# Two graph layers on one core: the order of work taken from a model of time for all engines

## The chip, the cores and the metric

The kernel runs on one core of one Trainium2 chip. The metric is device time in microseconds of one execution. Within the core, TensorE (PE) does the matrix products and transposes, ScalarE (ACT) the exponentials, Gelu and most copies out of PSUM, VectorE (DVE) masks, products, sums and statistics, GpSimd (POOL) a power of -1/2 on small tiles and the issue of one kind of load, and SyncE (SP) issues the other loads and the stores. Each engine takes its instructions in the order in which they were written, so the order of writing is the schedule.

## What is computed

Sixteen graphs of 1024 nodes with 256 features go through two layers. Layer 0 is graph attention with 4 heads of 64 features; layer 1 is masked attention with 8 heads of 32 features and an MLP 256 to 1024 to 256. Cut to what matters:

```python
# layer 0
h = einsum('bnd,hde->bhne', x, W)
weight = leaky_relu(sum over t of (adj == t+1) * (e_src[t][:, None] + e_dst[t][None, :]))
attention = softmax(where(adj == 0, -1e9, weight))
out = layernorm_per_head(relu(attention @ h + bias) + h)
x = layernorm(x + out)
# layer 1
n = layernorm(x) * gamma1 + beta1          # serves as query, key and value
a = softmax(where(adj > 0, n @ n.T / sqrt(32), -inf)) @ n
x1 = x + a
y = layernorm(x1) * gamma2 + beta2
x = layernorm(x + x1 + gelu(y @ W1 + b1) @ W2 + b2)
```

With the adjacency of these inputs only one edge type occurs, and the kernel uses this (a general path exists for other inputs and isn't taken).

## The kernel before

The work is two streams of instructions, written as Python generators. A step of a stream writes some instructions and yields a number, its cost in microseconds of PE time as the author reckoned it.

*Stream 0, layer0,* goes over the 16 batches. First `prepare`: for pairs of node blocks of 128 rows it transposes x (`transpose_rows`, L259, copied by ACT L262), transposes the adjacency into a byte mask (`turn_mask`, L327 on PE, L328 on ACT), multiplies with the weights (L354), lets ACT take parts of the product (L355 to L360), and leaves the value tile to a small chain, `values0` (L378, L379 on DVE). Then `attention0`: 16 steps, each for one half of the nodes (512 queries), one head and four key blocks; `weights` (L406, four DVE instructions) for the next step are written just after the products (L421) of this one. Once in two heads `spread_factor` (L395 on PE, L397 on ACT) makes a factor for the next pair. After the last step of a head two chains begin: `divide0` (L456 on DVE, L459 on ACT) and `after0` (L467 to L537), which adds h, normalises each pair of heads, and at the fourth head adds x, normalises the row, transposes it and leaves what layer 1 needs: x1, the values v1 and the transposed keys nT.

*Stream 1, layer1,* is one batch behind. `attention1` has 32 steps, each for 512 queries, four heads and one key block: `exponentials` writes four logit products into four PSUM banks (L559) and four exponentials (L564), `masked` multiplies the step before with the mask (L570, two DVE instructions), and `products` (L577, L584) takes the step before that one. After the eighth key block, `heads_out` (L619 to L635) divides and transposes, and after the second group of heads `finish1` (L646 to L664) adds x1, takes the statistics of four blocks (L225, L226), a power on POOL (L220), scales on ACT (L236) and transposes into yT. Then `mlp`: L682 on PE with Gelu L689 on ACT, L696 on PE for the chunk before, and one chain `last_norm` (L728 to L738) for each block of 128 rows, which ends with the store.

*What sets the order.* Three things. `COURSE` says how far layer 0 should be at each point of layer 1 (from 1.0 batch ahead at the start to 1.45 at the end of attention 1 and to 2.0 some 18 units before the end of the MLP); the main loop writes the next step of layer 0 if it is behind that course, otherwise of layer 1. The chains stand aside: a chain's part yields a wait, and `advance` writes its next part once the reckoned clock has moved that far. `complete` writes all that is left of a chain at once, where its result or its PSUM bank is needed: `bank0` does this for the readers of one of the two side banks, `finish_norms` for the norms of a half. `half(1)`, first needed at the fifth step of attention 1, is such a place.

The PSUM pools are `ps_s` (four banks), `ps_a` (two side banks, acc0 and acc1) and `ps_o` (two).

Of the kernel before, what the change touches and what calls it, by code (L numbers as in the profile page):

```python
# [31 lines left out]
F32 = mybir.dt.float32  # L32
# [7 lines left out]
P = 128  # L40
# [8 lines left out]

@with_exitstack  # L50
def fast_path(
# [24 lines left out]
    nc = tc.nc  # L76
# [23 lines left out]
    one = ctx.enter_context(tc.tile_pool(name="one", bufs=1))  # L100
    two = ctx.enter_context(tc.tile_pool(name="two", bufs=2))
    three = ctx.enter_context(tc.tile_pool(name="three", bufs=3))
    four = ctx.enter_context(tc.tile_pool(name="four", bufs=4))
    six = ctx.enter_context(tc.tile_pool(name="six", bufs=6))
    small = ctx.enter_context(tc.tile_pool(name="small", bufs=3))
    ps_s = ctx.enter_context(tc.tile_pool(name="ps_s", bufs=4, space=PSUM))
    ps_a = ctx.enter_context(tc.tile_pool(name="ps_a", bufs=1, space=PSUM))
    ps_o = ctx.enter_context(tc.tile_pool(name="ps_o", bufs=2, space=PSUM))
# [7 lines left out]
    make_identity(nc, ident)  # L116
# [73 lines left out]

    def later_weights():
# [5 lines left out]
        yield 6.0  # L197
        nc.sync.dma_start(w1_sb, w1.rearrange("(c p) f -> p c f", p=P))
        nc.sync.dma_start(w2_sb, w2.rearrange("(c p) d -> p c d", p=P))
        yield 24.0  # L200
# [11 lines left out]
        yield 3.5  # L212
# [10 lines left out]
    def statistics(src, mv):  # L223
        st = small.tile([P, 6], F32, name="st")
        nc.vector.bn_stats(st, src)  # L225
        nc.vector.bn_aggr(mv, st)  # L226
# [14 lines left out]
    def bank0(shape, dtype=F32):  # L241
# [4 lines left out]
        return ps_a.tile(shape, dtype, name=f"acc{i}"), banks0[i]  # L246
# [26 lines left out]
    clock = [0.0]  # L273
    chains = []

    def begin(chain, wait):
        chains.append([clock[0] + wait, chain])

    def run(item):
        wait = next(item[1], None)  # L280
        if wait is None:
            chains.remove(item)
        else:
            item[0] = clock[0] + wait

    def advance(cost):
        clock[0] += cost
        for item in list(chains):
            if item[0] <= clock[0]:
                run(item)  # L290

    def complete(chain):

        for item in list(chains):
            if item[1] is chain:
# [22 lines left out]
    def prepare(b, hb, esr, v0, dinv, mask):  # L318
# [18 lines left out]

        for k in range(0, NB, GB):
# [5 lines left out]
            yield 0.45  # L344
            turn_mask(k)
            yield 0.5
# [4 lines left out]
            for g in range(GB):  # L351
                ph, bank = bank0([P, D + 2 * H0])
# [5 lines left out]
                bank["readers"] = [values0(v0[:, k + g, :, :], ph)]  # L358
                begin(bank["readers"][0], 1.0)
                nc.scalar.copy(hb[-1][:, (k + g) % BPH, :], ph[:, 0:D])  # L360
                yield 0.9
                if g == 0:
                    turn_mask(k + 1)
                    yield 0.5
            turning = turn_sources(esr[:, k * P : (k + GB) * P])
# [903 lines left out]
```

## Time and profile before

| | before |
|---|---|
| median of three runs | 3697.59 us (3694.15 to 3701.16) |
| the profiled execution | 3704.23 us |
| its span | 3702.3 us |
| its mean granted PE clock | 0.978 |
| instructions | 142339 |
| first part, layer 0 of batch 0 alone | 0 to about 145 us |
| last part, layer 1 of batch 15 alone | from about 3523 us |

Profile lines give, for a chain row, the start in us, the length in us, the engine, the tile and the line of the kernel, and the number of records merged. Each fp32 product has two records. A line of waits names who waited for whom, then the total in us, the number of times and the longest. A busy PE is not a PE at its peak, since matmuls overlap in the record.

### The profile page before, as it was taken

Reading aid. Unit: us, or ns where it says so; the run is one execution under the profiler, and the core shown is the slowest. Engines: PE = TensorE matmul, PEld = TensorE weight load, DVE = VectorE, ACT = ScalarE, POOL = GpSimd, SP = SyncE. Lnnn points to the kernel's source line nnn. Section 1 sums busy time; section 2 is a strip of 40 time slices with the busy share of each in tenths; the row PEclk is TensorE's granted clock in tenths of the full one; section 3 lists DMA queues with packets and bytes.
Section 4 is the critical chain, followed back from the end, with each engine's and each line's share of the span. In section 5 each row is a group of like instructions: output and inputs, shape, how many; then the busy total and the mean of one; then the engine's idle time right before and its main releaser. Section 6 shows DMA issues by size and latency. Waiting matters only on the chain.

```text
span 3702.3 us, 142339 instructions
## 1 busy us (share of the span) xinstructions
PE 3487.3 (94%) x64673; PEld 2358.5 (64%) x64673; DVE 2857.4 (77%) x4882; ACT 2274.1 (61%) x5084; POOL 410.2 (11%) x392
## 2 busy tenths in 40 slices
PE   6799999999999999999999999999999999999998
PEld 5457576575756758566575765757657575675846
DVE  6787786877778787787877878788787877878774
ACT  3655757567475664757657475575756747566464
POOL 1101011010110101011020110101101011010100
PEclk9899999999999999999999999999999999999999
DMA  4101102011020110201102010110201102010000
GB/s 101 36 14 29 33 12 43 8 33 28 14 45 7 38 23 19 42 11 36 17 25 37 11 39 14 29 33 12 43 8 36 26 13 46 6 37 9 15 7 14
DMA packets 77525, 97.30 MB, mean 26 GB/s; under 512 B 9072, under 2 KB 59760, under 8 KB 76912
## 3 DMA queue, kind: packets, MB, share of 16 engines
q0 software_dynamic: 18432, 33.56, 6.4%
q1 hardware_dynamic: 56896, 53.50, 4.7%
q8 instruction: 508, 8.32, 0.9%
q10 hardware_dynamic: 1584, 1.05, 0.1%
q14 instruction: 105, 0.86, 0.1%
HBM read 104.87 MB, written 16.78 MB: 33 GB/s over the span
## 4 chain that ended last, share of the span: by engine, by line
PE 76%; DVE 16%; ACT 6%; issue 2%; DMA 0%; POOL 0%; ACTq 0%; POOLq 0%; DVEq 0%
PE ps L559 17%; PE po L577 13%; PE acc L421 11%; PE po L696 9%; PE ps L682 8%; PE po L584 7%; DVE p L406 3%; PE acc L354 3%; DVE st L225 2%; PE acc L259 2%; PE acc L327 2%; DVE p L570 1%; ACT relu L459 1%; DVE mv L226 1%; DVE o L646 1%
## 5 line engine op out<-in xcount | busy, mean ns | idle before, releaser
L570 DVE TENSOR_TENSOR p<-p,mask 128x1024 f32<-128x1024 f32 x1024 | 1202.7, 1220 | 245.1 <-ACT p L564 240.7
L564 ACT ACTIVATE p<-ps 128x512 f32<-128x512 f32 x2048 | 1071.1, 632 | 286.3 <-PE ps L559 283.2
L559 PE MATMUL ps<-nT 32*128 32x512 f32 x4096 | 761.7, 648 | 24.4 <-ACT cb L397 17.2
L406 DVE SCALAR_TENSOR_TENSOR p<-cb,dinv,mask 128x512 f32<-128x512 f32 x1024 | 698.4, 744 | 6.8 <-ACT cb L397 6.8
L421 PE MATMUL acc<-v,p 128*64 128x65 f32 x16384 | 575.6, 228 | 71.4 <-DVE p L406 63.4
L421 PEld LDWEIGHTS acc<-v,p 128*64 128x64 f32 x16384 | 526.6, 141 | 148.3 <-DVE p L406 71.8
L584 PEld LDWEIGHTS po<-v,p 128*32 128x32 f32 x32768 | 396.4, 110 | 321.1 <-issue 238.0
L577 PE MATMUL po<-p,v 128*32 128x512 f32 x2048 | 550.7, 613 | 2.4 <-DVE p L570 2.4
L577 PE MATMUL po<-p,unit 128*32 128x512 f32 x2048 | 550.0, 613 | 0.0
L682 PE MATMUL ps<-yT,w_sb 128*128 128x256 f32 x2048 | 487.5, 386 | 0.0
L696 PE MATMUL po<-w_sb,hid 128*128 128x256 f32 x2048 | 480.0, 385 | 0.0
L689 ACT ACTIVATE hid<-ps,b_sb 128x256 f32<-128x256 f32 x512 | 233.1, 474 | 351.2 <-PE ps L682 350.7
L682 PEld LDWEIGHTS ps<-yT,w_sb 128*128 128x128 f32 x2048 | 380.5, 191 | 64.5 <-issue 11.4
L696 PEld LDWEIGHTS po<-w_sb,hid 128*128 128x128 f32 x2048 | 386.1, 192 | 54.2
L584 PE MATMUL po<-v,p 128*32 128x33 f32 x32768 | 390.2, 198 | 4.2 <-issue 3.3
L559 PEld LDWEIGHTS ps<-nT 32*128 32x128 f32 x4096 | 265.4, 186 | 186.6 <-ACT p L564 62.0
L577 PEld LDWEIGHTS po<-p,v 128*32 128x32 f32 x2048 | 78.4, 108 | 371.6 <-DVE p L570 202.0
L220 POOL TENSOR_TENSOR r<-v,mhalf 128x1 f32<-128x1 f32 (+1 forms) x160 | 148.5, 928 | 756.8 <-DVE v L732 304.2
L328 ACT ACTIVATE mask<-acc,shift_c 128x1024 uint8<-128x1024 bf16 x128 | 148.1, 1157 | 82.3 <-PE acc L327 81.8
L220 POOL TENSOR_TENSOR r<-v1s,mhalf 128x4 f32<-128x4 f32 x32 | 61.9, 1933 | 1171.5 <-DVE v1s L651 1171.5
L459 ACT ACTIVATE relu<-acc,ranges 128x64 f32<-128x64 f32 x512 | 119.1, 323 | 109.2 <-DVE ranges L456 109.2
L236 ACT ACTIVATE z<-z,t,r 128x256 f32<-128x256 f32 x128 | 81.6, 638 | 162.2 <-DVE t L230 160.7
(121 smaller groups left out, 3087.6 us busy)
## 6 DMA issues: line engine op xcount, KB each, us to landing
ak<-in_adj_dram POOLq DMA_DIRECT2D x128, 256.0 KB, 3.9
xk<-in_x_dram SPq DMA_DIRECT2D x64, 256.0 KB, 2.8
xl<-in_x_dram SPq DMA_DIRECT2D x32, 512.0 KB, 3.9
out_dram<-z SPq DMA_DIRECT2D x128, 128.0 KB, 1.7
w_sb<-in_L_gnn_W_dram SPq DMA_DIRECT2D x2, 1024.0 KB, 6.7
v<-in_L_gnn_a_src_dram SPq DMA_DIRECT2D x2, 320.0 KB, 4.7
v<-in_L_gnn_a_dst_dram ACTq DMA_DIRECT2D x1, 320.0 KB, 4.5
xl<-in_L_gnn_a_dst_dram ACTq DMA_DIRECT2D x1, 320.0 KB, 4.7
```

What stands on the lines that cost most here:

```text
L220: nc.gpsimd.tensor_tensor(r, src, mhalf[:, :n], op=OP.pow)
L406: nc.vector.scalar_tensor_tensor(p[:, i, :], cb[:, hd % PAIR, :], dinv[:, j2 + i, hd : hd + 1], mask[n][:, j2 + i, :], op0=OP.max, op1=OP. ...
L421: nc.tensor.matmul(av[at : at + TILE, q, :], ps[i // 2][:, i % 2, q * P + at : q * P + at + TILE], v0[:, j4 + i, hd, :], start=j4 + i == 0 ...
L459: nc.scalar.activation(t[:, q, :], av[:, q, 0:HO], AF.Relu, scale=rinv[:, q : q + 1])
L559: nc.tensor.matmul(tiles[e], of_keys[q, quad, keys], of_queries[q, quad, :], start=True, stop=True)
L564: nc.scalar.activation(p[:, i, :], tiles[e + i], AF.Exp, scale=SCALE1)
L570: nc.vector.tensor_mul(p, p, mask[n][:, jb, None, :].to_broadcast([P, PAIR, HALF]))
L577: nc.tensor.matmul(moved[at * Q : (at + 1) * Q, :], v, ps[0][:, e, :], start=jb == 0, stop=jb == NB - 1)
L584: nc.tensor.matmul(held[at : at + Q, q, e, :], ps[1][:, e, q * P + at : q * P + at + Q], values[:, hd, :], start=jb == 0 and e == 0 and q ...
L682: nc.tensor.matmul(ph, w1_sb[:, c, f * P : (f + 1) * P], yT[:, c, q * P : (q + GB) * P], start=c == 0, stop=c == DC - 1,)
L689: nc.scalar.activation(hid[f // 4][:, f % 4, :], ph, AF.Gelu, bias=b1_sb[:, f : f + 1], scale=1.0)
L696: nc.tensor.matmul(po, hid[f // 4][:, f % 4, g * P : (g + 1) * P], w2_sb[:, f, :], start=f == 0, stop=f == FC - 1,)
```

## The change

No operation is removed or added; what is written on the engines is the same work in another order. `nc` becomes a `Pace`, which passes every instruction on to the real `nc` and keeps, in Python, a reckoned time for each engine: when it is free, when each tile is written, and when it was last read. The costs are formulas for each engine. `Ring` stands for a tile pool: it knows which tiles are still in use, and before a buffer is taken again it completes the chains that use the old tile.

A chain's part no longer yields a wait but the engine it will run on, and what it needs: tiles, or functions that give a time. `advance` writes it once these are ready by the time that the engine gets there. A stream's step yields its cost, as before, and what its next step needs; the main loop follows the same `COURSE`, but takes the other stream where the chosen one is late by over 0.3 us more than the other, as long as layer 0 stays within `SLACK` (0.12 of a batch) of the course.

```diff
+class Ring:
+    def tile(self, shape, dtype, name, passing=False):
+        taken = self.taken.setdefault(name, [])
+        if len(taken) >= self.bufs:
+            self.pace.settle(taken[-self.bufs])
...
+    def ready(self, name, count=1):
+        taken = self.taken.get(name, [])
+        return max([self.pace.through(t) for t in taken[-self.bufs :][:count] if len(taken) >= self.bufs] + [0.0])
...
+class Pace:
+    LATENCY = {"tensor": 0.2, "scalar": 0.2, "vector": 0.12, "gpsimd": 0.2, "sync": 4.0}
...
+    def cost(self, engine, op, aps, kwargs):
+        n = max(a.free_size() for a in aps)
+        if engine == "tensor":
...
+                t = aps[0].free_size() * (4 if double else 1) / 2400 * (array[0] / P) * (max(array[1], 32) / P)
+            if array != self.array:
+                self.array, t = array, t + 0.1
+            return t
...
+            return t + (0.13 + n / 1450 if aps[1].space == PSUM else 0.2 + n / 1050)
+        if engine == "vector":
+            return 0.17 if n <= 16 else 0.075 + n / 960
+        return 0.35 + 0.2 * n
...
+        start = max([self.free[engine], self.read.get(out, 0.0)] + [self.written.get(i, 0.0) for i in ins if i != out])
+        end = self.free[engine] = start + self.cost(engine, op, aps, {**kwargs, "func": args[2] if len(args) > 2 else None})
+        self.written[out] = max(self.written.get(out, 0.0), end + self.LATENCY[engine])
...
-    nc = tc.nc
+    nc = Pace(tc.nc)
...
-    def begin(chain, wait):
-        chains.append([clock[0] + wait, chain])
+    def begin(chain, engine, *needs):
+        for n in needs:
+            if not callable(n):
+                uses(chain, n.tensor.name)
+        chains.append([chain, engine, needs])
...
-    def advance(cost):
-        clock[0] += cost
-        for item in list(chains):
-            if item[0] <= clock[0]:
-                run(item)
+    def advance():
+        for _ in range(2):
+            for item in list(chains):
+                if item in chains and when(item[2]) <= max(nc.now(), nc.free[item[1]]):
+                    run(item)
...
-                begin(relu, 2.3)
-                begin(norms[b, n, hd], 3.8)
-            yield 2.0
+                begin(relu, "vector", av)
+                begin(norms[b, n, hd], "vector", lambda: math.inf if waits(relu) else 0.0, t)
+            yield (2.0, *ps, *([bank0_ready] if j4 == NB - 4 else []))
...
-            yield 2.5
+            yield (2.5, logits_ready, *ready.get(i - LAG + 1, ()), *([outs_ready] if jb == NB - 1 else []))
...
-        yield 2.0
-        yield 2.0
+        yield "vector", r
         t = minus_mean(mv[:, :, 0], r, BPH)
-        yield 1.5
+        yield "scalar", t
         scale_shift(o, o, t, r, BPH)
         for g in range(0, BPH, GB):
-            yield 2.5
+            yield "tensor", o, side_ready
             transpose_rows(yT[:, :, g * P : (g + GB) * P], o[:, g : g + GB, :])
...
-                begin(chain, 6.0)
-                begin(bias, 20.0 + 20.0 * n)
+                begin(chain, "vector", lambda: math.inf if waits(heads) else 0.0, o)
+                begin(bias, "vector", at_time(nc.now() + 24.0), x1)
...
+    SLACK = 0.12
...
     while any(streams):
-        lead = streams[0] and (place[0][0] + place[0][1] / WORK0 < wanted() or not streams[1])
-        which = 0 if lead else 1
-        cost = next(streams[which], None)
+        (b0, done0), target = place[0], wanted()
+        at0 = b0 + done0 / WORK0
+        which = 0 if streams[0] and (at0 < target or not streams[1]) else 1
+        if all(streams):
+            late = [when(n) - nc.now() for n in needs]
+            other = 1 - which
+            allowed = at0 < min(target + SLACK, place[1][0] + 2.05) if other == 0 else at0 > target - SLACK
+            if allowed and late[which] > max(late[other], 0.0) + 0.3:
+                which = other
```

All other waits of chains (`divide0`, `after0`, `heads_out`, `last_norm`, `later_weights`, `values0`, `turn_sources`) are exchanged in the same way: the number gives way to an engine and the tiles or banks that the part needs. `after0` has one more place to stop, ahead of v1. In `prepare` the readers of a bank are no longer completed by `bank0`; `Ring` does that, and `turn_sources` of a pair of blocks is completed ahead of the next pair's first product.

## The prediction

> **What bounds the kernel now.** I read the page's shares first, then the chain that ended last over the whole span (to find the period), then that chain and the order-of-time view over one batch, and last the waits.
>
> ```profile
> PE 3487.3 (94%) x64673; PEld 2358.5 (64%) x64673; DVE 2857.4 (77%) x4882; ACT 2274.1 (61%) x5084; POOL 410.2 (11%) x392
> PEclk9899999999999999999999999999999999999999
> PE 76%; DVE 16%; ACT 6%; issue 2%; DMA 0%; POOL 0%; ACTq 0%; POOLq 0%; DVEq 0%
> ```
>
> PE looks full, but the chain gives it only 76%, so a quarter of the span ends on DVE, ACT or issue. In the chain, the first L559 matmuls of a batch lie at 358.62 and, 14 batches on, at 3522.99: a period of 226.0 us. The program has three parts: 0 to 145 us (layer 0 of batch 0 alone), 15 periods with both layers, and 180 us from 3523 (layer 1 of batch 15 alone). DMA and POOL are on no path that counts.
>
> What PE needs in a period I take from undisturbed rows of the chain: an attention-1 step is 1.07 (L559) + 1.00 (L577) + 0.56 (L584) = 2.63 us, times 32 = 84.2; an attention-0 step 2.02, times 16 = 32.3; the MLP 3.45 per 16 records, 256 records = 55.2; L354 8 x 0.95, L327 8 x 0.55, 20 groups of transposes (L259, L635, L536) at about 0.56, L372 and L395 3.3 together. Sum 198. So 28 us of each period is lost, though the busy row hides most of it. DVE needs 2857/16 = 179 us, so neither engine forbids a period near 200.
>
> Three stretches of the chain, batch from 1938.7 to 2167.9 (start, length, what):
>
> ```profile
> 1968.19 1.00 PE po L577 x8
> 1969.19 0.56 PE po L584 x57
> 1969.75 1.70 PE ps L559 x7
> 1971.44 1.00 PE po L577 x8
> ...
> 2008.17 1.24 DVE o L646
> 2009.43 0.44 DVE st L225
> 2011.86 1.13 DVE x L653
> 2013.47 1.01 PE acc L327 x8
> 2014.48 1.87 PE acc L354 x4
> 2016.34 2.02 PE ps L559 x8
> ...
> 2080.60 0.70 DVE s L477
> 2081.32 0.69 DVE hb L478
> 2082.01 0.67 DVE p L406
> 2082.73 3.33 PE acc L421 x64
> 2086.06 2.53 PE ps L682 x8
> ```
>
> First, an attention-1 step with nothing of layer 0 beside it: L559 takes 1.70 instead of 1.07, because it writes the four logit banks that the exponentials are just emptying. Second, the first part of finish1 (L646 to L653), a block of some 4.7 us on DVE, stands ahead of values0 (L378), whose bank L327 wants. Third, DVE stands waiting for relu, does the head sum, and only then the weights that L421 wants. The waits name the same pairs:
>
> ```profile
> DVE hb L467 <- ACT relu L459: 152.6, 104, 3.0
> PE acc L421 <- DVE p L406: 63.4, 36, 3.2
> PE acc L327 <- DVE z L378: 50.5, 15, 3.4
> ```
>
> **The Trainium skill.** "Perfetto Trace Analysis", section Identifying the Most-Contended Engine, says that matmul busy time is no measure of headroom because matmuls are pipelined. The trace agrees: 94% busy, 76% of the chain. "TensorE: Matmul & The Clock Gate", Part 1, says that an idle window of about 3.4 us halves the clock, and that about as long a busy one restores it. The trace agrees with the halving: after 3.36 us of idle before 2013.47, L327 takes 1.01 instead of 0.55, L354 1.87 instead of 0.95, L559 2.02 instead of 1.07. But idle of 1.84 us before 2082.73 also made L421 3.33 instead of 2.02, so the measured stalls decide: the slow stretch costs about as much again as the stall. "PSUM — Partial Sum Buffer", Specifications, gives 8 banks; the kernel's pools hold 4 + 2 + 2, so no order of work can have more in flight than now.
>
> **The change, part by part.** *Instructions.* None is removed or added; Pace, Engine and Ring run while the program is written and keep times in Python. So everything comes from order. DVE, ACT and PE totals stay. The table loads (L689, L397, L564: 91 of 1283 ns, 7.3 us per batch on ACT) follow the alternation of streams, which I take as unchanged; five more per batch would be 6.4 us on an engine that is 61% busy, so I price it at 0, at most 1 us.
>
> *Chains placed when their engine would not wait.* The fixed waits go; a part is written once the model says that its inputs are there when the engine gets to it. That removes in-order blocking like DVE's 1.5 us before each hb L467 and ACT's 160.7 us before L236 of z. It does not split finish1's first part, nor the head sum.
>
> *Streams chosen by readiness.* The course stays the default; the other stream goes first if the chosen one is more than 0.3 us late and later than the other, within 0.12 of a batch (5.6 units of 47, about three attention-0 steps). A late step no longer holds PE while an MLP unit (1.73 us of PE, needing only Gelu) is ready.
>
> The losses of this batch, and what I take as recovered (lowest to highest in brackets):
> (a) About eight lone attention-1 steps, 8 x 0.63 = 5.0. The model puts the four L559 one after another (0.213 each), while the trace shows them ending together after about 1.1, so it sees the next step late by some 0.1, under the 0.3. Recovered 1 (0 to 2).
> (b) The finish1 block: 3.36 idle + (0.46 + 0.92 + 0.95 + 0.31) slow = 6.0. Attention-1 can be put ahead of L327, 2.6 us of PE work; after it, the masked weights (L570) are behind the same block. Recovered 3 (0 to 6).
> (c) 2020 to 2028: ACT does scale_shift of o (1.94) ahead of the exponentials and cb; 7.5 us for some 4.6 of PE work, 2.9 lost. Recovered 1.5 (0 to 2.9).
> (d) Start of the MLP, 2069 to 2088: 0.65 issue + 1.84 idle + 1.31 + 0.80 slow = 4.6. MLP units are ready there. Recovered 3.5 (1 to 4.6).
> (e) 2117 to 2126, the same pattern: 1.64 idle + 1.23 + 1.0 slow = 3.9. Recovered 3 (1 to 3.9).
> (f) Batch change, 2162 to 2173: ACT's scale_shift (2.07), its table load (1.28) and the exponentials in a row; 7.1 us for 4.8 of PE work, plus slow clock, about 3. Recovered 1 (0 to 2).
> Sum 13 (2 to 21).
>
> *What comes late instead.* Layer 0 may be held back by the 0.12. Its last head ends at 2146.6 now, and its norm chain runs until the L537 copies at 2182, forced at the fifth attention-1 step, when the second half's keys are needed. Summed from rows (relu 0.93, hb 2 x 0.69 + 0.42, sq 0.63, sum 0.68, POOL 2.0, three products 3.1, statistics 2.7, POOL 1.65, scale_shift 2.07, transposes and copies 3.4), the chain can't be shorter than about 19 us where it now takes 35, so up to 10 us of delay can be carried if its parts are written promptly; they are looked at only after each stream step of 2 to 4 us, twice per look. I take 4 us per batch given back here and through errors of the model (its attention-0 step is 1.83 against 2.02, attention-1 2.35 against 2.63). Ends: 0 to 17, the rival below. The other queues that parts move past: out stores and xl loads on SP go with their parts, and SP waits for ACT z for 2382 us in all with nothing hurt; POOL's adjacency loads stay with turn_mask, three masks of some 9.5 us ahead of use and 3.9 us to landing; a power queued behind one that waits for PE is a risk that the kernel already has.
>
> Net 13 - 4 = 9 us per period, times 15 = 135. Startup: chains on DVE beside its weights (L406 is 698/16 = 44 us of the 103 us after 42) stop blocking, and layer 1 may start at 0.88 of the batch; the forced chain (9.2 us of PE idle before 141.35) stays: 8 (0 to 25). The tail has no second stream: 2 (0 to 5). Sum 145. The profiled execution took 3704.23 (span 3702.3), so 3559; it stands 6.6 above the median shown, so against the median 3553. I say 3555.
>
> **Rivals.** *Bursts stay bursts* (0.25): the parts are placed better, but PE has nothing else to do during DVE blocks, since every alternative also needs DVE or a bank. Only the MLP's (d) and (e) come back, 6.5, less 4: 2.5 x 15 + 5 = 43, 3655. For it: DVE is at 77%, and in the chain it holds most of what PE doesn't. Against: MLP units need no DVE.
> *Nearly all comes back* (0.12): 18 per period and 15 at the start, 285, 3413. For it: 198 of PE and 179 of DVE. Against: (a) and the size of finish1.
> *Layer 0's norms arrive late* (0.20, slower): held back by its slack, the last head ends some 5 us later, the chain crosses more looks, and at the fifth attention-1 step of each batch the forced rest (scale_shift 2.07, transposes and copies 3.4, the wait for statistics and POOL about 5) stands before PE: 10 us and about 3 of slow clock, against a gain of 9: 4 x 15 = 60, 3758. It decides from the point where stall and slow clock there exceed 9 to 13 us. For it: already now the chain ends only by force at that step. Against: ten MLP steps still lie behind the last head.
>
> **How the numbers follow.** The forecast has 0.43, with 3490 to 3620 as its own range. A measurement here can tell about 0.2%, 7 us. Faster: 0.43 + 0.12 + most of 0.25 = 0.77; same 0.03; slower 0.20. Range 3435 to 3725: it cuts about half of the 0.12 below and two thirds of the 0.20 above.
>
> **What would show it.** Right: period near 217; "PE acc L421 <- DVE p L406" and "PE acc L327 <- DVE z L378" well under 63 and 50; DVE's wait before hb L467 under half of 152.6; L421 at 3.3 gone from the chain while lone L559 rows of 1.7 stay. Wrong: a PE idle at the fifth attention-1 step of each batch, released by the norm's nT or sq, or a period over 225.

## The result, and the profile after

The changed kernel takes 3724.24 us (3720.37 to 3724.94, four runs) against 3696.61 us for the kernel before on the same chip. The ratio is 1.0071, with a 95% interval of 1.0054 to 1.0089: slower, by some 28 us, where 3555 had been forecast. The profiled execution has a span of 3718.2 us, at a mean granted clock of 0.970 (before 0.978). The period is 227.2 us (before 226.0). The two profiled executions differ by only 16 us, since the one before is slower and the changed one faster than its median; the 15 periods account for all of these 16.

All instructions of the changed kernel pass through one helper, so each row names L61, and rows are told apart by their tiles: ps<-nT is L559, po<-p,v and po<-p,unit L577, acc<-ident,xk and acc<-ident,sq the transposes of L259 (xk for the next batch's input, sq for the norm chain), acc<-ident,nT the v1 transposes of L536, acc<-identb,ak L327, acc<-w0e,xT L354, acc<-v,p L421, ps<-yT,w_sb L682, po<-w_sb,hid L696.

First the page of the changed kernel, busy times and engines of the chain that ended last:

```profile
PE 3430.7 (92%) x64673; PEld 2312.9 (62%) x64673; DVE 2856.3 (77%) x4882; ACT 2288.2 (62%) x5084; POOL 406.6 (11%) x392
...
PE 73%; DVE 16%; ACT 8%; issue 2%; DMA 0%; POOL 0%; ACTq 0%; DVEq 0%; POOLq 0%
```

DVE is busy for as long as before, ACT for 14 us more, PE for 57 us less (3430.7 after 3487.3) in a longer span. PE's share of the chain fell from 76 to 73%, and ACT's rose from 6 to 8%. So PE waits more than before. For whom, the waits of PE in the changed kernel say (total in us, times, longest), with one line of the kernel before below them:

```profile
PE acc L61 <- ACT mask L61: 58.8, 19, 10.0
PE po L61 <- DVE p L61: 55.0, 40, 5.0
PE acc L61 <- DVE p L61: 51.9, 17, 3.4
...
PE acc L61 <- DVE z L61: 4.5, 7, 0.7
```

```profile
PE po L577 <- DVE p L570: 2.4, 1, 2.4
```

Of the pairs shown before, that of L327 for z has all but gone (4.5 after 50.5), and PE's wait of L421 for p seems to have stayed (51.9 after 63.4). But it is another wait now: before, 52 of the 63 us lay in the MLP; in the changed kernel none does, and 45 of the 52 stand right behind finish1's block on DVE in attention 1, once in each of the 14 whole periods:

```profile
2946.79 2.67 PE L61 MATMUL acc<-v,p 128*64 128x65 f32 x64 [3.19 <-DVE p L61]
```

Two pairs are new, and weigh more than what went: a side bank waits for ACT's mask 19 times, about once a period, and L577 for masked weights 40 times, 55.0 us where it was 2.4.

Where they lie shows best by stage, from the first L559 rows of a batch to its first L682 rows (attention 1), and from there to the next batch (the MLP). In the mean of the 14 whole periods, attention 1 takes 132.7 us before and 144.5 in the changed kernel, the MLP 93.3 and 82.7. The MLP got shorter and attention 1 longer by a little more. Both ends of the long stretch have a reading of their own. Its beginning, in order of time on PE (start, length, operation; in brackets the idle time before and its releaser):

```profile
2864.74 0.62 PE L61 MATMUL acc<-identb,ak 128*128 128x128 bf16 x8
2868.60 1.12 PE L61 MATMUL acc<-ident,sq 128*128 128x128 f32 x4 [3.24 <-ACT mask L61]
2869.51 1.06 PE L61 MATMUL acc<-ident,nT 128*128 128x128 f32 x4
2870.83 1.12 PE L61 MATMUL acc<-ident,nT 128*128 128x128 f32 x4 [0.26 <-ACT nT L61]
2872.88 2.13 PE L61 MATMUL acc<-w0e,xT 128*128 128x264 f32 x4 [0.94 <-ACT v L61]
2874.94 2.09 PE L61 MATMUL ps<-nT 32*128 32x512 f32 x8
```

The next batch's preparation (ak, then w0e,xT) is cut by the whole rest of the previous half's norm chain: its second transposes, then both v1 transposes, each waiting for the copy of the one before. Nothing of attention 1 stands between them. PE idles 3.24 us and then runs at half speed: w0e,xT takes 2.13, ps<-nT 2.09 (1.07 undisturbed). At the undisturbed durations, the rows that start between 2855 and 2875 are some 11 us of work in 20 (the first expectation below says 8). Counted in this way from 4 us ahead of a batch's first L559 rows to 18 us behind, PE loses 9.5 us at each batch change, and lost 2.3 before (means of 14).

The end of the stretch, the chain of the same kernel from 2984:

```profile
2984.06 4.92 DVE p L61 x6
...
2991.44 1.21 DVE p L61
...
2993.25 5.19 DVE p L61 x5
...
2999.04 1.41 DVE p L61 x2
...
3000.54 2.26 DVE p L61 x2
...
3003.60 9.27 PE ps L61 x44
3012.87 2.02 PE acc L61 x64
```

DVE carries the end here: it masks attention 1's weights and makes layer 0's weights (L406) for six attention-0 steps, where before there were four in this stretch. From 2934 to 3003.6 DVE is busy for 65.8 of 69.6 us, 95% (before, the last 69.6 us ahead of the MLP have 85% in the mean):

```profile
2934.00:3003.60 69.60, 61.78 (x1674) 35.31 (x1673) 65.79 (x92) 39.66 (x84) 3.96 (x2) 1.00 0.01 3
```

(The columns are the length, then busy time with the number of instructions for PE, PEld, DVE, ACT and POOL, then the granted clock, the DMA share and GB/s.) Then comes the reverse: 44 records of L682 in a row, 9.27 us in which layer 0 is made to stand until the course has caught up.

### The profile page after: what moved, and what is told of

Read it like the earlier page. It is cut to its first block, busy times and chain, and to the rows that moved or that the text cites. A ratio compares the mean times of both kernels' runs of the same rounds, so it can differ in the third digit from the quotient of the medians.

```text
span 3718.2 us, 142342 instructions
## 1 busy us (share of the span) xinstructions
PE 3430.7 (92%) x64673; PEld 2312.9 (62%) x64673; DVE 2856.3 (77%) x4882; ACT 2288.2 (62%) x5084; POOL 406.6 (11%) x392
## 4 chain that ended last, share of the span: by engine, by line
PE 73%; DVE 16%; ACT 8%; issue 2%; DMA 0%; POOL 0%; ACTq 0%; DVEq 0%; POOLq 0%
PE ps L61 28%; PE po L61 26%; PE acc L61 19%; DVE p L61 11%; ACT p L61 3%; DVE hb L61 1%; ACT sq L61 1%; DVE st L61 1%; ACT nT L61 1%; DVE o L61 1%; ACT x L61 1%; ACT mask L61 1%; ACT relu L61 1%; ACT L61 1%; ACT cb L61 1%
## 5 line engine op out<-in xcount | busy, mean ns | idle before, releaser
L61 DVE TENSOR_TENSOR p<-p,mask 128x1024 f32<-128x1024 f32 x1024 | 1201.7, 1220 | 237.3 <-ACT p L61 237.3
L61 ACT ACTIVATE p<-ps 128x512 f32<-128x512 f32 x2048 | 1056.3, 605 | 369.6 <-PE ps L61 369.2
L61 DVE SCALAR_TENSOR_TENSOR p<-cb,dinv,mask 128x512 f32<-128x512 f32 x1024 | 699.1, 746 | 36.1 <-ACT cb L61 35.7
L61 PE MATMUL ps<-nT 32*128 32x512 f32 x4096 | 699.6, 655 | 24.6 <-ACT p L61 14.6
L61 PE MATMUL acc<-v,p 128*64 128x65 f32 x16384 | 556.3, 227 | 54.0 <-DVE p L61 51.9
L61 PE MATMUL po<-p,v 128*32 128x512 f32 x2048 | 547.8, 610 | 55.0 <-DVE p L61 55.0
L61 PEld LDWEIGHTS po<-v,p 128*32 128x32 f32 x32768 | 387.2, 110 | 332.3 <-issue 202.4
L61 PEld LDWEIGHTS acc<-v,p 128*64 128x64 f32 x16384 | 517.4, 141 | 114.7 <-DVE p L61 55.6
L61 PE MATMUL po<-p,unit 128*32 128x512 f32 x2048 | 547.6, 610 | 0.0
L61 ACT ACTIVATE hid<-ps,b_sb 128x256 f32<-128x256 f32 x512 | 239.3, 474 | 421.1 <-PE ps L61 421.0
L61 PE MATMUL po<-w_sb,hid 128*128 128x256 f32 x2048 | 473.2, 383 | 0.0
L61 PE MATMUL ps<-yT,w_sb 128*128 128x256 f32 x2048 | 471.8, 382 | 0.0
L61 PEld LDWEIGHTS po<-w_sb,hid 128*128 128x128 f32 x2048 | 382.8, 190 | 74.8 <-issue 22.8
L61 PEld LDWEIGHTS ps<-yT,w_sb 128*128 128x128 f32 x2048 | 381.7, 190 | 51.9
L61 PE MATMUL po<-v,p 128*32 128x33 f32 x32768 | 387.1, 198 | 3.6
L61 PEld LDWEIGHTS po<-p,v 128*32 128x32 f32 x2048 | 77.9, 108 | 424.1 <-DVE p L61 316.1
L61 PEld LDWEIGHTS ps<-nT 32*128 32x128 f32 x4096 | 224.5, 187 | 146.1 <-issue 51.4
L61 POOL TENSOR_TENSOR r<-v0s,mhalf 128x8 f32<-128x8 f32 x64 | 129.0, 2016 | 1012.9 <-DVE v0s L61 1012.9
L61 POOL TENSOR_TENSOR r<-v,mhalf 128x1 f32<-128x1 f32 (+1 forms) x160 | 145.9, 915 | 621.6 <-DVE v L61 487.2
L61 PE MATMUL acc<-w0e,xT 128*128 128x264 f32 x512 | 157.8, 433 | 28.9 <-ACT mask L61 13.3
L61 ACT ACTIVATE relu<-acc,ranges 128x64 f32<-128x64 f32 x512 | 119.5, 329 | 93.2 <-DVE ranges L61 93.2
L61 POOL DMA_DIRECT2D ak<-in_adj_dram x128 | 68.8, 538 | 968.0 <-PE acc L61 955.5
```

The lines of the kernel that those rows point to most:

```text
L61: return method(*args, **kwargs)
```

## The experiments

Four theories. A: a ring that takes a buffer again completes *everything* left of a chain that ever touched it, even a part that reads it no more, and so puts whole chains ahead of PE's work. B: the choice by readiness lets layer 0 run ahead in attention 1, where DVE is already full. C: the model's times are too short, so that "ready" is said too soon. D: finish1's first part is a stall by itself, whatever places it. The rival to all of them is that the losses are those of the parts' placing as such, so that chains placed by the model are slower in any order of the streams.

**A: what the rings complete.** The first run takes the banks of the transposes, which are read at once by the copies after them, as `passing`, a flag that `Ring.tile` already has: they are then not bound to the running chain. `side_bank` hands the flag on, and the v1 transposes use it in the same way. The second adds that a chain that has begun isn't completed for its relu tile.

```diff
-    def bank0(shape, dtype=F32):
+    def bank0(shape, dtype=F32, passing=False):
...
-        return ps_a.tile(shape, dtype, f"acc{i}"), banks0[i]
+        return ps_a.tile(shape, dtype, f"acc{i}", passing), banks0[i]
...
-        pt = side_bank([P, DC, GB, P])
+        pt = side_bank([P, DC, GB, P], True)
...
-            if chain not in running:
+            if chain not in running and not (tile.startswith("relu") and chain in begun):
                 complete(chain)
```

> The changed kernel, but a side bank that a chain fills and empties within one part is no longer counted as still used by that chain, so taking the bank again no longer forces the rest of the norm chain (transposes, x1, v1) at the start of each batch. Theory A (forced completion at the batch change is what ate the gain: 20 us from 2855.8 to 2875 for about 8 us of PE work, 12 lost where the kernel before lost some 3): 6 to 9 us less per period, 3590 to 3635. Theory B (layer 0 pulled ahead into attention 1, where DVE is the bound, ate it): the batch change moves little of the total, 3700 to 3735. Theory C (the model's times are too short, so readiness is misjudged everywhere): 3700 to 3735 as well.

> As the one before, and the relu tile is no longer counted as used by after0 once its first part, the only one that reads it, is written. Theory A: again a little less than f1_bank, 3580 to 3630. Theories B and C: 3690 to 3735.

Measured: 3664.16 us, ratio 0.9904 (0.9883 to 0.9924), and 3656.01, 0.9882 (0.9859 to 0.9906). The first edit alone takes 60 us from the changed kernel, 4 per period, and makes it faster than before. It is less than the 6 to 9 per period that theory A expected, and both runs miss their ranges. The same place, PE of the kernel with the first edit in order of time (the rows of L577 and L584 left out):

```profile
2816.42 0.78 PE L61 MATMUL acc<-identb,ak 128*128 128x128 bf16 x8
2816.99 2.07 PE L61 MATMUL acc<-w0e,xT 128*128 128x264 f32 x4
2818.99 1.69 PE L61 MATMUL ps<-nT 32*128 32x512 f32 x8
...
2822.17 0.66 PE L61 MATMUL acc<-ident,sq 128*128 128x128 f32 x4
...
2825.83 0.66 PE L61 MATMUL acc<-ident,nT 128*128 128x128 f32 x4
2826.61 1.16 PE L61 MATMUL acc<-w0e,xT 128*128 128x264 f32 x4
...
2829.03 0.66 PE L61 MATMUL acc<-ident,nT 128*128 128x128 f32 x4 [1.26 <-ACT v L61]
```

w0e,xT follows its mask at once, and the norm chain's transposes come one by one between attention-1 steps. PE's wait for the mask falls from 58.8 to 6.8 us, and the loss at the batch change from 9.5 to 5.4, which is all of the 4.2 us by which the period fell. That the bank's binding is the cause at this spot is shown, since it alone was changed. Not all went: every later kernel that keeps the model's chains or the choice of streams still loses about 5 to 6 us there, and those with neither 2.4 to 2.6. Why is not shown.

**B: running ahead.** Both runs keep the repaired rings. One follows the course alone; the other lets the choice hold layer 0 back but never send it ahead.

```diff
-            allowed = at0 < min(target + SLACK, place[1][0] + 2.05) if other == 0 else at0 > target - SLACK
+            allowed = False
```

```diff
-            allowed = at0 < min(target + SLACK, place[1][0] + 2.05) if other == 0 else at0 > target - SLACK
+            allowed = other == 1 and at0 > target - SLACK
```

> As f2_settle, but the stream is always that of the course (no choice by readiness); chains are still placed by the model. Theory B: attention-0 steps in the attention-1 stretch go back from 6 to 3 or 4, the DVE-bound stretch of some 70 us before the MLP shrinks by 10 or more, the MLP gets its waits on DVE back: 20 to 90 us less than f2_settle. Theory A: no less than f2_settle, rather 20 to 100 more, since choosing by readiness helped the MLP. Theory C: within 20 of the kernel before, 3680 to 3720.

> As f2_settle, but readiness may only put layer 1 first (layer 0 may fall behind the course by 0.12, never run ahead of it). Theory B: the best of the four, 40 to 110 us less than f2_settle. Theory A: equal to f2_settle within 20. Theory C: equal to f3_settle_course within 20 and both near 3700.

Measured: 3633.85 us, 0.9819 (0.9798 to 0.9840), and 3631.91, 0.9817 (0.9790 to 0.9843). Both are some 22 to 24 us below the run that may run ahead, less than the 40 expected of the second; holding back adds only 2, which these runs can't tell from nothing. PE's waits, ahead allowed and then not:

```profile
PE acc L61 <- DVE p L61: 55.6, 20, 3.2
PE po L61 <- DVE p L61: 54.5, 44, 2.2
```

```profile
PE acc L61 <- DVE z L61: 31.0, 22, 1.8
...
PE acc L61 <- DVE p L61: 7.6, 5, 2.2
...
PE po L61 <- DVE p L61: 2.2, 1, 2.2
```

The waits for weights go from 110 to 10 us; what is left is L327's wait for z behind the finish1 block. Counted while the order is written, the changed kernel takes layer 0 against the course some 390 times, all of them in attention 1. By stage, with running ahead and without, both with repaired rings: attention 1 takes 139.5 and 130.8 us, the MLP 82.7 and 90.0. Running ahead gains 7.3 us in the MLP and pays 8.7 in attention 1.

**Chains alone, streams alone.** The next run leaves the rings as changed and follows the course alone: the chains' part of the change without the streams' part.

```diff
-            allowed = at0 < min(target + SLACK, place[1][0] + 2.05) if other == 0 else at0 > target - SLACK
+            allowed = False
```

> The changed kernel with the stream always that of the course; forced completion as in the change. Against f3_settle_course (3634) it differs by the forced completion alone. Theory A (forcing whole norm chains costs PE time wherever a ring comes round, not only at the batch change): 3 to 8 us per period more than f3, 3680 to 3750. If forcing mattered only together with the choice of streams: 3625 to 3650. Against the changed kernel (3724) theory B says that it is faster, below 3715.

Measured: 3644.68 us, 0.9848 (0.9831 to 0.9864). The chains' part alone makes the kernel 56 us faster than before (some 40 of them by what seems a side effect, see below), so the rival falls. It also shows that the two parts spoil each other: the unrepaired rings cost 11 us here (against 3633.85) and 68 with the free choice of streams. That this is because the choice alternates preparation and attention-1 steps one for one, and so takes the side banks again sooner, is argued from the trace, not shown.

The other side: chains placed by fixed waits as before, on a clock that counts the steps' costs, in the new frame with repaired rings. Three kernels: the course alone, the free choice, and the choice without running ahead.

```diff
+    WAITS = {
...
+        "values0": (1.0,),
...
+        "divide0": (2.3, 0.3),
...
+        "heads_out": (0.0, 0.0, 1.5, 1.5),
+        "finish1": (6.0, 4.0, 1.5, 2.5, 2.5),
...
-                if item in chains and when(item[2]) <= max(nc.now(), nc.free[item[1]]):
+                if item in chains and item[1] <= clock[0]:
```

> A control: tile rings as in f2_settle, chains placed by the fixed waits of the kernel before, streams by the course alone. Nearly the order of the kernel before: 3685 to 3715.

> The control with the change's choice of streams by readiness (0.12 ahead and behind): the second part of the change alone. Theory B (running ahead into attention 1 costs by itself): 15 to 60 us more than the control. Rival (the choice is good by itself and hurt only together with forced completion): 0 to 60 less than the control.

> The control with the choice of streams, layer 0 never ahead of the course. Theory B: 15 to 60 us less than h2_streams_alone. My prediction's parts (d) and (e), stalls in the MLP that a ready MLP unit fills, come from this choice: 40 to 100 less than the control. Rival (with chains placed well those stalls go anyway, as f3 and f4 are equal, and with fixed waits the choice finds little): 0 to 30 less than the control.

Measured: 3657.78 us, 0.9892 (0.9873 to 0.9912); 3672.28, 0.9927 (0.9909 to 0.9945); 3640.84, 0.9849 (0.9828 to 0.9870). The last two speak for B with other chains: the free choice stands 14 above the course (the intervals touch), without running ahead it stands 17 below. They also decide about the MLP's stalls, which the prediction took to be filled by this choice: 40 to 100 us were expected of it, and 17 came, or 2 where the model places the chains. The first was a miss, and an important one: as a copy of the old order it should have stood within 20 us of the kernel before, and it stood 40 below.

**What the control owed its 40 us to.** In the frame, taking the accumulator again completes `heads_out`, so its transposes (L635) are written ahead of the next step's products rather than behind them, and the divisions after them go with them. This spot was moved alone, in the kernel before, and then finish1's first part was also split in three and begun 3 us earlier:

```diff
             if jb == 0:
+                if ends:
+                    complete(ends.pop())
                 moved = ps_o.tile([P, HALF], F32, name="po")
...
                 begin(chain, 0.0)
+                ends.append(chain)
```

```diff
-                begin(chain, 6.0)
+                begin(chain, 3.0)
...
             statistics(o[:, g, :], mv[:, g, :])
+            if g == 1:
+                yield 2.0
...
         r = power(v, BPH, "r1")
+        yield 2.0
         nc.vector.tensor_add(x1, x1, o)
         yield 2.0
-        yield 2.0
```

> The kernel before, with one edit: what is left of heads_out is written as soon as the accumulator is taken again, one step earlier than before. If this spot is what the control with fixed waits owed its 40 us to, 3650 to 3675 with a period of 223 us. If the 40 us came from the many other small shifts (norm chain, order on ACT), 3685 to 3700.

> The same, and finish1 begins 3 instead of 6 us later with its first part in three pieces, one step apart (sum and two statistics; two statistics and the power; x1). If the block in attention 1 is a stall of its own, whatever places the chains (3.3 us per period with the model), another 40 to 50 us below the run without it: 3610 to 3630. If only the placing by the model lets the pieces fall between the masked weights, no more than 15 us below it.

Measured: 3651.43 us, 0.9885 (0.9861 to 0.9909), and 3600.08, 0.9737 (0.9721 to 0.9753). This spot of heads_out alone gives as much as the control did, which speaks for it as the source of the 40 us. PE in the kernel with that edit alone, at the block that the prediction showed at 2008 to 2016:

```profile
1986.17 0.66 PE L639 MATMUL acc<-ident,oT 128*128 128x128 f32 x4
...
1992.86 0.61 PE L327 MATMUL acc<-identb,ak 128*128 128x128 bf16 x8 [1.81 <-DVE z L378]
1993.31 1.11 PE L354 MATMUL acc<-w0e,xT 128*128 128x264 f32 x4
1994.35 1.14 PE L559 MATMUL ps<-nT 32*128 32x512 f32 x8
```

(L639 is the L635 of before.) After the transposes PE has the products of that step, 1.00 + 0.56 us, more to do until it comes to L327, while DVE's block begins as soon after them as it did. PE idles 1.81 us instead of 3.36. In the batch that the prediction showed, the rows behind the longer wait ran at half speed, but this was not the rule. Two batches of the kernel before:

```profile
2013.47 1.01 PE L327 MATMUL acc<-identb,ak 128*128 128x128 bf16 x8 [3.36 <-DVE z L378]
2014.27 2.07 PE L354 MATMUL acc<-w0e,xT 128*128 128x264 f32 x4
...
2693.22 0.61 PE L327 MATMUL acc<-identb,ak 128*128 128x128 bf16 x8 [3.36 <-DVE z L378]
2693.66 1.11 PE L354 MATMUL acc<-w0e,xT 128*128 128x264 f32 x4
```

The same wait occurs 15 times before. Behind 5 of them L354 takes 2.07 us, behind 10 it takes 1.11. With the edit the wait is 1.80 to 1.81 us 15 times, and L354 takes 2.06 once. "TensorE: Matmul & The Clock Gate", Part 1, of the Trainium skill says that an idle window of about 3.4 us halves the clock; here a wait just under that was followed by half speed in 5 cases of 15, and one of 1.8 us in one of 15. The waits over the whole program:

```profile
PE acc L421 <- DVE p L406: 63.3, 36, 3.2
PE acc L327 <- DVE z L378: 27.1, 15, 1.8
```

The first stands as it did, the second went from 50.5 to 27.1. The mean granted clock of the profiled execution goes from 0.978 to 0.985. Counted by the rows at undisturbed durations, PE's loss per period falls by 3.2 us, from 27.9 to 24.7, about the gain of 45: 2.4 in attention 1, where the wait became 1.6 shorter, and 0.8 in the MLP, where the order of the instructions is the same as before. There half speed has become rarer (41 us of the 14 whole periods before, 10 with the edit). So where half speed falls is part of the gain, and how much of this the edit causes was not tried.

**C and D: the model's times, and the block.** From the repaired rings without running ahead: one kernel cuts finish1's first part into four, one has costs fitted to the rows of the trace, one has both; a fourth sets layer 0's due time six units earlier in the MLP, to see whether the batch change is cured by an earlier norm chain.

```diff
+        yield "vector", at_time(nc.now() + 2.0)
         mv = small.tile([P, BPH, 2], F32, name="mv1")
         for g in range(BPH):
             statistics(o[:, g, :], mv[:, g, :])
+            if g == 1:
+                yield "vector", at_time(nc.now() + 2.0)
...
+        yield "vector", at_time(nc.now() + 2.0)
         nc.vector.tensor_add(x1, x1, o)
```

```diff
-                self.array, t = array, t + 0.1
-            return t
+                self.array, t = array, t + 0.15
+            return t + 0.0044
...
-            return t + (0.13 + n / 1450 if aps[1].space == PSUM else 0.2 + n / 1050)
+            return t + (0.13 + n / 1330 if aps[1].space == PSUM else 0.394 + n / 2080)
...
-            return 0.17 if n <= 16 else 0.075 + n / 960
+            return 0.17 if n <= 16 else 0.18 + n / 1024
...
-        self.written[out] = max(self.written.get(out, 0.0), end + self.LATENCY[engine])
+        row = engine == "tensor" and op == "matmul" and aps[1].shape[0] < P
+        self.written[out] = max(self.written.get(out, 0.0), end + self.LATENCY[engine] + (0.5 if row else 0.0))
```

```diff
-(WORK1 - 18.0, 2.0)
+(WORK1 - 24.0, 2.0)
```

> f4_settle_noahead, with the first part of finish1 (an addition, four statistics, an addition: 4.7 us on DVE without a break) cut into four parts, each written some 2 us of PE time after the last. Theory D (of what f4 still loses, the block in attention 1 is a stall of its own: 2857 to 2872 in f4, about 6 us per period with the slow clock): 4 to 6 us less per period, 3540 to 3575. Rival (DVE is loaded there anyway and the wait only moves to the next steps): 0 to 20 less, 3610 to 3635.

> f4_settle_noahead with the model's costs set to the durations of the trace (attention-0 step 2.02 instead of 1.83, array change 0.15, ACT 0.515 instead of 0.483 for an exponential and 0.517 instead of 0.444 for 256 elements, DVE 1.18 and 0.68 instead of 1.14 and 0.61, outputs of four row tiles 0.5 later). Theory C (wrong times misplace parts and streams): 30 us or more less, below 3602. Rival (the order hardly depends on costs that are all a tenth too low): 3615 to 3650.

> g2_split and g3_times together: if both act in different places, 3583 - 12 = 3571, within 12; if better times already spread the DVE block, about 3583; below 3555 would mean that they help each other.

> f4_settle_noahead with layer 0 due 24 units before the end of the MLP instead of 18, so that the norms of the last head are done before the batch changes. Theory A in its weaker form (what is left at the batch change, 12 us from 2784.2 to 2796 for about 4 of PE work, comes from the norm chain's end, scale_shift and nT, standing before the first exponentials on ACT): 3 to 6 us less per period, 3540 to 3590. Rival (attention-0 steps closer together make DVE the bound in the MLP and give it back): 3620 to 3660.

Measured: the split 3582.85 us, 0.9680 (0.9664 to 0.9696), 49 us below the kernel without it; the times 3619.71, 0.9781 (0.9765 to 0.9797), 12 below; both 3563.87, 0.9633 (0.9615 to 0.9650), the best of all; the earlier due time 3630.40, 0.9809 (0.9792 to 0.9825), no difference. So splitting the block gives more than any other edit here (3.3 us per period), and it does so without a model too: in the kernel before with heads_out moved, splitting and the earlier begin gave 51. The block occurs twice in a batch, once for each half of the nodes, and theory D named only the one in attention 1. In that kernel L327's wait for z, 27.1 us, is gone, and L421's wait, which lies for the most part in the MLP, falls from 63.3:

```profile
PE acc L421 <- DVE p L406: 36.7, 21, 3.2
```

By the rows, 0.7 us of the gain per period lie in attention 1 and 2.6 in the MLP. The model's times are too short (it reckons about 211 us for a period that takes 227), but setting them right is worth only 12 to 19 us, and what is left at the batch change isn't a matter of the due time (5.9 us are lost there with the earlier one, 5.4 without; the 12 us that its expectation names hold 8 us of work by the rows, not 4). The chain of the best kernel, by engine:

```profile
PE 86%; issue 4%; ACT 4%; DVE 3%; POOL 1%; DMA 0%; ACTq 0%; POOLq 0%; DVEq 0%
```

DVE's share of the chain is 3% where it was 16, at nearly the same busy time (2845.5 us after 2857.4).

## Why the prediction was wrong

By the ratios, each step against the one before it, at 3697 us: the frame with fixed waits -40 (heads_out's step, its spot by itself, in the kernel before, -42); chains placed by the model -27; the choice of streams, holding back only, -1; running ahead +24; what the rings complete +70. The sum is the measured +26 because of the way it is made, which is no check. Each step is uncertain by about 10 us. The last two depend on the order in which they are undone: from the changed kernel, taking away the choice of streams first gives 82, and the rings then 11. Together they are 93 or 94 in either order.

PE's loss in each period (its length less the work at the undisturbed durations, 198 us), by stage, in the mean of the 14 whole periods:

| kernel | attention 1 | MLP |
|---|---|---|
| before | 19.0 | 8.9 |
| frame with fixed waits, the course alone | 16.5 | 7.9 |
| chains by the model, rings repaired, the course alone | 18.7 | 4.1 |
| the same, streams chosen, holding back only | 17.1 | 5.5 |
| the same, running ahead too | 21.7 | 2.3 |
| the changed kernel | 26.8 | 2.3 |

*The steps that failed.* The prediction had 9 us per period gained, 13 less 4; 1.7 were lost (26 / 15). Both terms failed. The 13 is the larger miss: the gains come to 4.5 (68 / 15), and 2.7 of these are heads_out's step, which the prediction did not have, so that 1.9 came from what it priced. It added up (a) to (f) as if each could be had without a cost in another stage. The table shows otherwise: the model's chains took 3.8 from the MLP's loss and put 2.2 on attention 1's; the choice of streams, which was to fill (d) and (e), gave 2 us in the whole program without running ahead, and with it clears the MLP and pays more in attention 1.

The other term is "4 us per batch given back". It priced layer 0 "held back" by the 0.12, and the model's errors. The changed order instead lets layer 0 *ahead*, and completes chains by the rings: 6.3 us per period in all (94 / 15), 1.6 and 4.7 in the order of the list, 5.5 and 0.7 in the other. The prediction named the 0.12 as a bound for "the other stream", whichever it is, but followed only one side, and it put at nothing what the rings complete. This term decides the direction: with 4 instead of 6.3 the kernel would have stood about where it stood before.

*Readings that were off.* The losses were read in the longest of the 14 whole periods, which loses 31 us by the rows where the mean is 28. Behind the wait of 3.36 us half speed came 5 times in 15, so (b) is nearer 4 than 6. And L421 behind the wait of 1.84 us takes 2.67 in 10 of 15 batches and 3.1 or more in 5; the 2.67 is the time of the four L406 instructions that make its weights (2.73), so half of the 1.31 that (d) adds for L421 is DVE's pace and not the clock.

*The slower rival* had the place right and the mechanism wrong. It said a forced norm chain at the batch change, about 10 us and then the slow clock. Measured: PE loses 9.5 us there, half-speed rows included (before 2.3). But it isn't forced at the fifth attention-1 step by the keys that are needed there, nor because the last head came late; it is forced at the third step of preparation by a side bank that it no longer reads. The diff says this in one sentence ("completes the chains that use the old tile"), and the prediction passed over what "use" covers.

*The gain of 13, term by term:*

- (d) and (e), the MLP's stalls, were recovered as said: the MLP's loss fell from 8.9 to 2.3. But this was bought by moving layer 0 into attention 1, where the loss rose from 19.0 to 26.8.
- (b), the finish1 block, was said to give back 3 of 6. In the changed kernel L327's wait went, because other work stood there, and came back as L421's wait behind the same block (3.2 us, shown above); L577's waits lie elsewhere, at the end of attention 1. Only splitting the block, in both halves, gave 3.3 per period. "It does not split finish1's first part" stood in the prediction as a remark, and was worth more than the whole change.
- (a): in the changed kernel more went than the 1 us said; its chain has two or three lone rows of about 1.70 in a batch instead of eight, because preparation is spread between attention-1 steps one for one. With running ahead taken away nine are back, and this version is faster: they were not worth what it took to fill them.
- (c), ACT's scale of o ahead of the exponentials, is in the chain of every batch before (1.9 us) and of none in the changed and the repaired kernels, so it went; the sum was still as above.
- (f), the batch change, was to give 1 and cost about 7 (9.5 after 2.3).
- Start and tail, 10 us in the forecast, moved by less than 3.

Of the signs named ahead: the period over 225 came, and the PE idle released by the norm chain's copies came at the third step of preparation; DVE's wait before hb fell from 152.6 to 86.2, not under half. L421's wait moved from the MLP into attention 1, and went only when running ahead was taken away.

*Bursts stay bursts*, the second rival, is the nearest to what the parts do without the two faults: 3655 was said, 3644.68 (chains alone) and 3656.01 (rings repaired, all else as changed) were measured. The numbers agree for the wrong reason, since both hold the 40 us of heads_out, which the prediction did not have.

Open: why forced completion costs six times as much under the free choice as under the course; why 5 to 6 us stay lost at the batch change; and how much of the placing's 27 us comes from which chain.

## What to carry to other kernels

Before pricing what an order-making planner gains, ask of each of its rules what it forces at once: completing a chain for a buffer that it has finished with put a whole chain ahead of TensorE, and cost 68 us in this kernel, more than the placing gained; where the same rule happened to force a chain at the right place (heads_out), it seems to have gained some 40. Readiness on one engine is no reason to start work early if that work loads the engine that is full in this stage; a share over the whole program (DVE 77%) hides a stretch where it is 95%. A stall that is filled in one stage has to be priced with what its filling takes from another. And look for the longest uninterrupted block on a helper engine first: two small edits of the old order by hand, one chain's end written a few instructions sooner and one block cut in three, gave 96 us, and the best kernel with a model of time for all engines stands 36 below that.

## What was not expected of the hardware

Writing a chain's last transposes and divisions ahead of one step's products instead of behind them took 1.2% off the whole program (0.9885, 0.9861 to 0.9909).

The length of one gap does not decide whether half speed follows: the same wait of 3.36 us ahead of the same rows was followed by half speed in 5 batches of 15 (2.07 us for L354) and by full speed in 10 (1.11), and behind a wait of 1.84 us L421 was slowed beyond DVE's pace in 5 of 15 (3.1 us or more against 2.67). In each of these traces, half speed comes in stretches of 3.41 us and whole multiples of it, which all begin on one grid of that width (the end of the span cuts the last). In the 14 whole periods there are 28 such widths before, 45 in the changed kernel, 15 with heads_out moved and none in the best kernel. So the same gap can count or not by where it falls; that this is what decided is not shown, and what else does was not tried.
